# Moving the edge search for the last node tiles into the head of a graph layer, and starting its adding DMAs there

## The chip, the cores and the metric

The kernel runs on one core of one Trainium2 chip, as a single launch. The metric is the device time of one execution in microseconds (us); lower is better. Engines are named as the profile names them: PE (TensorE matmul), PEld (its weight loads), DVE (VectorE), ACT (ScalarE), POOL (GpSimd), and SP (SyncE), whose queue SPq issues most of the DMAs.

## The reference

One layer of a graph network on 3125 nodes with 256 channels and 103,125 directed edges (50,000 random pairs in both directions, and a loop on every node), sorted by destination. Cut to what matters:

```python
def _L0_gnn_ref(x, edge_index, ...):
    src, dst = (edge_index[0], edge_index[1])
    agg = jax.ops.segment_sum(x[src], dst, num_segments=N)     # N = 3125
    h = jax.nn.relu(agg @ W_rel + b_rel + x @ W_root)          # 256 -> 512
    gates = h @ W_ih.T + b_ih + b_hh
    i, f, g, o = jnp.split(gates, 4, axis=-1)
    c = jax.nn.sigmoid(i) * jnp.tanh(g)
    h_lstm = jax.nn.sigmoid(o) * jnp.tanh(c)
    return h_lstm @ W_fc + b_fc

xn = _layernorm(x, axis=-1)
x = x + gnn(xn, edges) + mix(xn)          # mix: k^T v per head over all nodes
x = x + ffn(_layernorm(x, axis=-1))       # top 2 of 8 experts, 256 -> 1024 -> 256, gelu
```

## The kernel before, in words

**Tiles.** The nodes lie in 25 tiles of 126 rows. The sum over edges is done in two ways. For the first 22 tiles (TA) it is a dense product: in the edge stage PE builds a 0/1 matrix `A` of source node by destination node, 252 destinations (a chunk) at a time, and multiplies the normalised nodes (as two parts, `hi` and `lo`) by it into `aggT`. A chunk has 14 builds: DVE writes two one-hot tiles `hr` and `hk` (line 477, two buffers each), PE multiplies them into a bank (483), ACT copies the bank into `A` (485). While the matmuls of one chunk run (796), the builds of the next are interleaved with them, bank by bank; there are 11 chunks, and `A0` for the first is built in the head.

For the last 3 tiles (TG) the sum is made by DMA: up to 60 times, for each tile, POOL issues an indirect DMA that gathers one source row for each of 126 nodes from `xn_dram` and adds it to an SBUF buffer (407, 180 such adds in all). Even ones add into `acc`, a view of `flat`, odd ones into `odds`.

**Head.** The nodes are loaded and normalised in five batches (`norm`), written to `xn_dram`, transposed (`turn`) and multiplied by W_root (`root`). Beside this, `find` looks up in the sorted edge list where the edges of each group of 6 nodes begin: DVE compares the first edges of all columns with the group's limit (282), POOL gathers the column found (290), DVE counts in it (296), POOL gathers 256 edges from there (305), and DVE turns them into keys (313 to 322) that are transposed for the builds. `find` is a generator that the code steps at chosen places.

**The last tiles' search.** `find_last` does the same for the 378 single nodes of the last three tiles: three compares over all columns (348), a gather (356), a check of the order of all edges (361, 362), three counts (366), a gather of 64 edges for each node (372), the hits (380), a PE matmul that adds up the counts of what went wrong (384), and the list `source` of rows to add (393 to 396). Before the change its first step stands at the end of the head, behind the last build of `A0` and the last `lo` split, and the other three in chunk 0 of the edge stage, beside banks 4, 8 and 10.

**Orders.** A scheduler places each engine's instructions; the code pins some of them. `then(ins, do, ...)` and `behind_(...)` run a step with its instructions queued behind given instructions on the same engine. In the edge stage a dictionary `queue` maps a chunk and a bank to the steps that stand beside it: the steps of the head mixer (`fetch`, which loads a batch `q` of `xn_dram` rows, `means`, `differences` and so on), `small_columns` and `router_rows`. In chunk 0 `fetch` stands at bank 7 and `means` (line 676, `hmean`) at bank 11, for the first batch. `next(adding)` issues an add beside some of the banks.

Of POOL's small work, `blank` (649, a row of zeros with an index in it) is stored by SP into `acc_dram` (652) and used for four fills of `xs_dram` (823); `heads` (640) masks the mixer's product; `tri`, `onesb`, `first`, `soon`, `token`, `valid`, `beyond` and `seen` serve the router.

**GNN chunks.** After the edge stage the nodes pass in seven chunks of up to four tiles (CUTS) through W_rel (1094), the gates (1104, four groups `m`), W_fc (1131) and the mixer's product (1134), then layer norms and the router, whose rows POOL scatters into `xs_dram` (1245). In each chunk the loop over `m` issues up to five adds per group, the first of which waits for the group's last matmul. The leftover adds are issued at the chunk that ends at tile 22 by `turned`: it adds `odds` to `acc` on DVE (1069), transposes the six blocks on PE (1073) and copies them on ACT into `accT`, which the last chunk reads in place of `aggT`. The experts' blocks (996, 1020) follow, and their rows are added into `out`.

Of the kernel before, what the change touches and what calls it, by code (L numbers as in the profile page):

```python
# [9 lines left out]
F32 = mybir.dt.float32  # L10
I32 = mybir.dt.int32
# [6 lines left out]
N = 3125  # L18
C = 256
# [20 lines left out]
TA = T - TG  # L40
GQ = 4
# [3 lines left out]
J = 60  # L45
SB = 256
# [24 lines left out]
def gps_layer(  # L71
# [21 lines left out]
    def ps_tr():  # L93
        return psum.tile([128, 512], F32, tag="tr", name="ps_tr", bufs=2)
# [42 lines left out]
    flat = main.tile([128, TG * C], F32, name="flat")  # L137
    acc = flat[:P].rearrange("p (m c) -> p m c", c=C)
    accT = flat[:, :KC * TG * P].rearrange("p (k n) -> p k n", k=KC)

    def agg_of(k, t0, t1):
        return aggT[:, k, t0 * P:t1 * P] if t0 < TA else accT[:, k, (t0 - TA) * P:(t1 - TA) * P]

# [99 lines left out]

    def find():
# [8 lines left out]
        for i in range(2):  # L253
            ends = sp.tile([128, NCP], F32, name="ends", tag="ends", bufs=3)
            nc.scalar.copy(ends, raw[:, i, :])
            for r in range(0, nr, 4):
                pt = ps_tr()
                m = min(4, nr - r)
                for j in range(m):
                    w = min(128, NCP - 128 * (r + j))  # L260
                    nc.tensor.transpose(pt[:w, 128 * j:128 * j + 128],
                                        ends[:, 128 * (r + j):128 * (r + j) + w], ident)
                whole_ = m if NCP >= 128 * (r + m) else m - 1
                if whole_:
                    nc.scalar.copy(rows[:, r:r + whole_, :, i],
                                   pt[:, :whole_ * 128].rearrange("p (r e) -> p r e", e=128))
                if whole_ < m:
                    nc.scalar.copy(rows[:left, r + whole_, :, i],
                                   pt[:left, whole_ * 128:m * 128])
# [10 lines left out]
        scr = sp.tile([128, NCP], F32, name="scr", tag="ends", bufs=3)  # L280
        for q in range(GQ):
            nc.vector.tensor_scalar(scr[:GP], firsts[:GP], limit[:, q:q + 1], None, op0=OP.is_lt, op1=OP.add,
                                    accum_out=below[:, q:q + 1])
# [11 lines left out]
        for q in range(GQ):  # L295
            nc.vector.tensor_scalar(scr[:GP, :128], near[:, q, :, 0], limit[:, q:q + 1], None,
                                    op0=OP.is_lt, op1=OP.add, accum_out=below[:, q:q + 1])
# [6 lines left out]
        for q in range(GQ):  # L304
            nc.gpsimd.indirect_dma_start(
                out=both[:, q].rearrange("p e o -> p (e o)"), out_offset=None,
                in_=ends_dram.rearrange("n e o -> (n e) o"),
                in_offset=bass.IndirectOffsetOnAxis(ap=begin_i[:, q:q + 1], axis=0))
        yield
# [30 lines left out]
    gathered = []  # L340

    def find_last():


        below = ep.tile([P, TG], F32, name="below2")
        for m in range(TG):
            scr = sp.tile([128, NCP], F32, name="scr2", tag="ends", bufs=3)
            nc.vector.tensor_scalar(scr[:P], firsts[:P], node[:, m:m + 1], None, op0=OP.is_lt,
                                    op1=OP.add, accum_out=below[:, m:m + 1])
        at = ep.tile([P, TG], F32, name="at2")  # L350
        nc.vector.tensor_scalar(at, below, -1.0, 0.0, op0=OP.add, op1=OP.max)
        at_i = ep.tile([P, TG], I32, name="at2_i")
        nc.vector.tensor_copy(at_i, at)
        near = ep.tile([P, TG, 128, 2], F32, name="near2")
# [5 lines left out]
        order = sp.tile([128, NCP], F32, name="order", tag="ends", bufs=3)  # L360
        nc.vector.tensor_tensor(order, raw[:, 0, :], behind, OP.is_gt)
        nc.vector.tensor_reduce(wrong[:, GQ:GQ + 1], order, AX.X, OP.add)
        yield
        hits = ep.tile([P, TG * JE], F32, name="hits2")
        for m in range(TG):
            nc.vector.tensor_scalar(hits[:, :128], near[:, m, :, 0], node[:, m:m + 1], None,
                                    op0=OP.is_lt, op1=OP.add, accum_out=below[:, m:m + 1])
        begin_i = ep.tile([P, TG], I32, name="begin2_i")
        nc.vector.scalar_tensor_tensor(begin_i, at, 128.0, below, op0=OP.mult, op1=OP.add)
        both = ep.tile([P, TG, JE, 2], F32, name="both2")  # L370
# [6 lines left out]
        yield  # L377
        mine = hits.rearrange("p (m e) -> p m e", e=JE)
        for m in range(TG):
            nc.vector.tensor_scalar(mine[:, m], both[:, m, :, 0], node[:, m:m + 1], None,  # L380
                                    op0=OP.is_equal)
        nc.vector.tensor_reduce(wrong[:P, GQ + 1:], mine[:, :, J], AX.X, OP.add)
        pw = ps_tr()
        nc.tensor.matmul(pw[:, :GQ + 2], ones, wrong, start=True, stop=True)
        total_f = const.tile([128, 1], F32, name="total_f")
        nc.vector.tensor_reduce(total_f, pw[:, :GQ + 2], AX.X, OP.add)
        off = const.tile([128, 1], F32, name="off")
        nc.vector.tensor_scalar(off, total_f, 1.0, float(FAR), op0=OP.min, op1=OP.mult)
        nc.vector.tensor_copy(total_i, total_f)
        yield  # L390


        nc.vector.scalar_tensor_tensor(mine, both[:, :, :, 1], -float(N), mine,
                                       op0=OP.add, op1=OP.mult)
        nc.vector.tensor_scalar(mine, mine, float(N), off[:P], op0=OP.add, op1=OP.add)
        nc.vector.tensor_scalar(source, mine, float(N), None, op0=OP.min)

    source = gw.tile([P, TG, JE], I32, name="source")

    def adds():  # L400

        for j in range(J):
            for m in range(TG):
                with ExitStack() as queued:
                    for one in added:
                        queued.enter_context(tc.issue_after(one.ins))
                    add = nc.gpsimd.indirect_dma_start(  # L407
                        out=(acc, odds)[j % 2][:, m, :], out_offset=None, in_=xn_dram[:, :],
                        in_offset=bass.IndirectOffsetOnAxis(ap=source[:, m, j:j + 1], axis=0),
                        compute_op=OP.add)  # L410
                added[:] = [add]
                yield add
# [84 lines left out]
    def then(ins, do, *of):  # L497

        with tc.issue_after(ins.ins):
            return do(*of)  # L500
# [20 lines left out]
    last = then(last, norm, 1)  # L521
    root(0)
    then(xts[-1][1], rounded, 0)
    then(last, next, steps)
    begun = pins.pop()
# [20 lines left out]
    keyed = pins.pop()  # L546
    listing = lambda: next(steps, None)
    root(3, *(GQ * [listing]))
    behind_((pins[0], evacs[-3]), norm, 4)
# [3 lines left out]
    one = lambda: next(parts)  # L553
    root(4, None, one, one)
    then(xts[-1][1], rounded, 4)
    next(parts)
    root(5, one, one, one)
    next(parts)
    stored = root(6, one, one, one)
    for part_ in parts:  # L560
        built = part_
    for b in range(2, T // TB):
        splits = then(built[1], split, b)
    last_steps = find_last()
    behind_((splits, built[1]), next, last_steps)
    found.close()
    nodes.close()
    adding = adds()

# [48 lines left out]
    odds = keep.tile([P, TG, C], F32, name="odds")  # L618
    for of in (acc, odds):
        nc.gpsimd.memset(of, 0.0)  # L620
# [18 lines left out]
    heads = keep.tile([128, 128], F32, name="heads")  # L639
    nc.gpsimd.memset(heads, 0.0)  # L640
    for i in range(128 // HC):
        nc.gpsimd.memset(heads[i * HC:(i + 1) * HC, i * HC:(i + 1) * HC], 1.0 / N)
# [3 lines left out]
    pkv = []  # L646

# [111 lines left out]
    queue = {(0, i): [(next, last_steps, None)] for i in (4, 8, 10)}  # L759
    queue[0, 9], queue[1, 3] = [(small_columns,)], [(router_rows,)]  # L760
    ADDS = 11
# [8 lines left out]
    with tc.tile_pool(name="odd", bufs=1) as op_:  # L770
        As = [A0, op_.tile([P, T, AC], F32R, name="A1")]
        for c, (d0, d1) in enumerate(chunks):
# [5 lines left out]
            def bank(i):  # L778
                built = next(parts, None)
                if built is None:  # L780
                    return
                with ExitStack() as queued:
                    for ins in built:
                        queued.enter_context(tc.issue_after(ins.ins))
                    for step, *of in queue.pop((c, i), ()):
                        step(*of)

                n = c * NB + i - ADDS
                if n >= 0 and n * 11 // 16 > (n - 1) * 11 // 16:
                    next(adding)  # L790
# [42 lines left out]
    with tc.If(total > 0):  # L833
        with tc.tile_pool(name="any", bufs=1) as ap_:
# [56 lines left out]
            nc.vector.tensor_tensor(acc, acc, ag, OP.add)  # L891
# [168 lines left out]
    with tc.tile_pool(name="gnn", bufs=1) as hp, tc.tile_pool(name="rt", bufs=2) as rp:  # L1060
# [4 lines left out]
        def turned():  # L1065

            for _ in adding:
                pass
            nc.vector.tensor_tensor(acc, acc, odds, OP.add)
            pts = [ps_tr() for _ in range(KC)]  # L1070
            for k in range(KC):
                for m in range(TG):
                    nc.tensor.transpose(pts[k][:, m * P:(m + 1) * P],
                                        acc[:, m, 128 * k:128 * k + 128], ident[:P, :P])
            for k in range(KC):
                nc.scalar.copy(accT[:, k, :], pts[k][:, :TG * P])

        def chunk(t0, t1, pending):
# [20 lines left out]
            for m in range(KH):  # L1099
# [10 lines left out]
                nc.scalar.activation(act[:, 1, :n], act[:, 0, :n], AF.Tanh)  # L1110
                nc.vector.tensor_tensor(hl[:, m, :n], act[:, 2, :n], act[:, 1, :n], OP.mult)
# [10 lines left out]
                if m == 2 and t1 == TA:  # L1122
                    with tc.issue_after(mm.ins):
                        turned()
# [357 lines left out]
```

## Time and profile before

| | us |
|---|---|
| median of 3 runs | 1094.63 |
| lowest and highest of them | 1090.86, 1095.67 |
| time of the profiled execution | 1092.31 |
| span in that execution's profile | 1090.5 |
| mean granted PE clock in it | 0.977 of full |

Stages in the profile: the head ends at 80.5 us, with the first matmul of the edge stage; the edge stage runs to about 320; the GNN chunks to about 710; the experts' blocks to the end.

The profile's lines give a start and a length in us, the engine, the source line, the operation and its tiles (output<-input), and in brackets the idle time of the engine just before, with what ended it. "SPq" and "POOLq" are the queues' own instructions. In tables by window the columns are the busy time of PE, PEld, DVE, ACT and POOL with counts, then the clock that PE was granted (PEclk, 1 is full), the share of the DMA engines and GB/s.

### The profile page before, as it was taken

Reading aid. Unit: us, or ns where it says so; the run is one execution under the profiler, and the core shown is the slowest. Engines: PE = TensorE matmul, PEld = TensorE weight load, DVE = VectorE, ACT = ScalarE, POOL = GpSimd, SP = SyncE. Lnnn points to the kernel's source line nnn. Section 1 sums busy time; section 2 is a strip of 40 time slices with the busy share of each in tenths; the row PEclk is TensorE's granted clock in tenths of the full one; section 3 lists DMA queues with packets and bytes.
Section 4 is the critical chain, followed back from the end, with each engine's and each line's share of the span. In section 5 each row is a group of like instructions: output and inputs, shape, how many; then the busy total and the mean of one; then the engine's idle time right before and its main releaser. Section 6 shows DMA issues by size and latency. Waiting matters only on the chain. (4 is left out here: it accounts for less than half of the span.)

```text
span 1090.5 us, 15243 instructions
## 1 busy us (share of the span) xinstructions
PE 1016.8 (93%) x5296; PEld 783.0 (72%) x5296; DVE 538.4 (49%) x1734; ACT 422.1 (39%) x918; POOL 563.8 (52%) x472
## 2 busy tenths in 40 slices
PE   6996999989999999999996899999999999999994
PEld 3466989889984545454553666788888888888883
DVE  5868778867831393929291734471112222222220
ACT  4462748467413242424351334542322222322221
POOL 2105888888706748787877030353443534344444
PEclk9998999999999999999998899999999999999997
DMA  8953999999624444966363210147767665766641
GB/s 269 312 182 85 246 288 295 283 216 277 99 115 106 78 108 82 270 118 128 78 128 79 70 60 15 54 158 254 241 223 253 215 223 203 264 217 210 205 149 41
DMA packets 142674, 188.03 MB, mean 172 GB/s; under 512 B 14371, under 2 KB 124978, under 8 KB 142462
## 3 DMA queue, kind: packets, MB, share of 16 engines
q1 hardware_dynamic: 103668, 140.56, 39.9%
q0 software_dynamic: 38080, 45.57, 21.0%
q8 instruction: 44, 0.72, 0.3%
q10 hardware_dynamic: 840, 0.83, 0.2%
q14 instruction: 42, 0.34, 0.1%
HBM read 128.72 MB, written 59.06 MB: 172 GB/s over the span
## 5 line engine op out<-in xcount | busy, mean ns | idle before, releaser
L1104 PE MATMUL ps_mm<-hT,wih 128*128 128x504 f32 (+1 forms) x672 | 258.8, 545 | 0.0
L1104 PEld LDWEIGHTS ps_mm<-hT,wih 128*128 128x128 f32 x672 | 127.5, 191 | 126.7 <-issue 90.2
L996 PE MATMUL ps_mm<-xe,w 128*128 128x256 f32 (+1 forms) x896 | 185.3, 364 | 0.0
L1020 PE MATMUL ps_o<-w,hf 128*128 128x256 f32 x832 | 184.9, 379 | 0.0
L407 POOL DMA_INDIRECT odds<-xn_dram,source x90 | 158.4, 1760 | 34.7 <-issue 25.2
L996 PEld LDWEIGHTS ps_mm<-xe,w 128*128 128x128 f32 x896 | 160.4, 190 | 20.3 <-issue 0.2
L407 POOL DMA_INDIRECT flat<-xn_dram,source x90 | 154.4, 1716 | 35.3 <-issue 24.9
L1020 PEld LDWEIGHTS ps_o<-w,hf 128*128 128x128 f32 x832 | 155.7, 190 | 19.9
L796 PE MATMUL ps_o<-A,hi 126*128 126x252 f32 x550 | 151.3, 308 | 0.6 <-ACT A L485 0.6
L998 ACT ACTIVATE hf<-ps_mm,sm 128x256 f32<-128x256 f32 (+1 forms) x160 | 72.3, 452 | 188.0 <-PE ps_mm L996 185.9
L796 PE MATMUL ps_o<-A,lo 126*128 126x252 f32 x550 | 137.6, 282 | 0.0
L485 ACT CAST A<-ps_mm 126x450 fp32r<-126x450 f32 x154 | 82.5, 536 | 96.2 <-PE ps_mm L483 94.5
L483 PE MATMUL ps_mm<-hk,hr 128*126 128x150 bf16 x924 | 93.0, 237 | 21.9 <-DVE hk L477 20.4
L974 POOL DMA_INDIRECT old<-out_dram,xs x52 | 53.7, 1032 | 112.3 <-issue 67.8
L796 PEld LDWEIGHTS ps_o<-A,hi 126*128 126x128 f32 x550 | 106.3, 193 | 2.6 <-ACT aggT L804 1.7
L796 PEld LDWEIGHTS ps_o<-A,lo 126*128 126x128 f32 x550 | 106.6, 194 | 0.0
L477 DVE TENSOR_TENSOR hr<-two,rowT 128x756 bf16<-128x756 bf16 x154 | 84.2, 547 | 42.4 <-PE ps_mm L483 41.7
L483 PEld LDWEIGHTS <-hr 128*126 128x126 bf16 x924 | 82.8, 141 | 30.1 <-DVE hk L477 26.4
L477 DVE TENSOR_TENSOR hk<-two,keyT 128x900 bf16<-128x900 bf16 x154 | 95.7, 621 | 0.0
L1106 ACT ACTIVATE act<-ps_mm,bg 128x504 f32<-128x504 f32 (+1 forms) x84 | 52.9, 634 | 104.7 <-PE ps_mm L1104 103.9
L1245 POOL DMA_INDIRECT xs_dram<-rows,at_i x50 | 50.7, 1013 | 65.3 <-DVE at_i L1243 50.0
L1023 DVE TENSOR_TENSOR y<-ps_o,b2s 128x256 f32<-128x256 f32 x52 | 22.0, 424 | 120.7 <-PE ps_o L1020 81.2
(290 smaller groups left out, 1149.9 us busy)
## 6 DMA issues: line engine op xcount, KB each, us to landing
w<-in_W_dram SPq DMA_DIRECT2D x56, 1024.0 KB
xs_dram<-blank SPq DMA_DIRECT2D x3, 7022.5 KB
xs_dram<-blank SPq DMA_DIRECT2D x1, 6757.5 KB
xs<-xs_dram SPq DMA_DIRECT2D x21, 265.0 KB
root_dram<-hr SPq DMA_DIRECT2D x8, 504.0 KB
root<-root_dram SPq DMA_DIRECT2D x4, 1008.0 KB
b2s<-in_b_dram SPq DMA_DIRECT2D x28, 128.0 KB
xn_dram<-xn SPq DMA_DIRECT2D x5, 630.0 KB
```

The lines of the kernel that those rows point to most:

```text
L407: add = nc.gpsimd.indirect_dma_start(out=(acc, odds)[j % 2][:, m, :], out_offset=None, in_=xn_dram[:, :], in_offset=bass.IndirectOffsetOnA ...
L477: row = nc.vector.tensor_tensor(to[:, :m], two[:, :, :w, :].to_broadcast([128, m, w, GH]), of[:, g:g + m, None, :].to_broadcast([128, m, w ...
L483: mm = nc.tensor.matmul(pa[:P, i * DT:(i + 1) * DT], hr[:, i, :, h], hk[:, i, :, h], start=(h == 0), stop=(h == GH - 1))
L485: copy = nc.scalar.copy(A[:, :, c0:c0 + m * D], pa[:P, :m * DT].rearrange("p (d t) -> p t d", t=T))
L796: last = nc.tensor.matmul(pg[k][:, :n], of[:, t, 128 * k:128 * k + 128], A[:, t, :n], start=(t == 0 and of is hi), stop=(t == T - 1 and of ...
L974: get = nc.gpsimd.indirect_dma_start(out=old[:, h, :], out_offset=None, in_=out[:most, :], in_offset=self.rows_(h), bounds_check=most - 1, ...
L996: mm = nc.tensor.matmul(pm, self.w1[:, k, 128 * m:128 * m + 128], self.xe[:, k, :], start=(k == 0), stop=(k == KC - 1))
L998: nc.scalar.activation(hf[:, m, :], pm, AF.Gelu, bias=b1s[:, m:m + 1])
L1020: mm = nc.tensor.matmul(po, hf[:, m, 128 * h:128 * h + 128], self.w2[:, m, :], start=(m == 0), stop=(m == KF - 1))
L1104: mm = nc.tensor.matmul(pm[:, :n], wih[:, k, i, 128 * m:128 * m + 128], hT[:, k, :n], start=(k == 0), stop=(k == KH - 1))
L1106: nc.scalar.activation(act[:, i, :n], pm[:, :n], AF.Tanh if gate == 2 else AF.Sigmoid, bias=bg[:, gate, m:m + 1])
L1245: put = nc.gpsimd.indirect_dma_start(out=xs_dram[:, :], out_offset=bass.IndirectOffsetOnAxis(ap=at_i[:, i:i + 1], axis=0), in_=rows[:, i, ...
```

## The change

- `find_last` is stepped from the head: its first step behind `norm(1)` and ahead of `find`'s second, its gather behind `find`'s gathers, its counts and second gather behind the keys and ahead of `norm(4)`, its last two steps beside builds 3 and 5 of `A0`; `split(2)` stands beside build 8, and splits 3 and 4 stay behind the last build. The scratch buffers of the searches are borrowed from `aggT`.
- `acc` holds both sums of each tile (six slots); it is cleared at the start of POOL's work. `odds`, `flat` and `accT` go.
- Six adds are issued before the edge stage, and then beside its banks from the first bank on, at 13 for 16 banks instead of 11 for 16 from bank 11 on.
- `turned` no longer adds on DVE. PE multiplies both sums of a tile with the identity into one accumulator, and ACT copies it into columns of `aggT` that were used up (WRAP). It stands behind the gates' last matmul, the last tanh and the last product of the chunk that ends at tile 22, instead of beside its third group.
- `heads` moves from the pool `keep` to the mixer's pool on the same side.

The diff, cut to its core:

```diff
+WRAP = max(t for t in CUTS if t <= TA)
+SUMS = 2
+NS = TG * SUMS
...
-    flat = main.tile([128, TG * C], F32, name="flat")
-    acc = flat[:P].rearrange("p (m c) -> p m c", c=C)
...
     def agg_of(k, t0, t1):
-        return aggT[:, k, t0 * P:t1 * P] if t0 < TA else accT[:, k, (t0 - TA) * P:(t1 - TA) * P]
+        w = WRAP if t0 >= WRAP else 0
+        return aggT[:, k, (t0 - w) * P:(t1 - w) * P]
+    acc = main.tile([P, NS, C], F32, name="acc")
+    nc.gpsimd.memset(acc, 0.0)
...
+    room = [NCP]
+    def borrowed(n):
+        room[0] += TG * n
+        return aggT.rearrange("p k n -> p (k n)")[:P, room[0] - TG * n:room[0]].rearrange(
+            "p (m n) -> p m n", m=TG)
+    def scratch(p, n=NCP):
+        return aggT.rearrange("p k n -> p (k n)")[:p, :n]
...
     def find_last():
...
-        nc.vector.tensor_copy(at_i, at)
-        near = ep.tile([P, TG, 128, 2], F32, name="near2")
+        yield nc.vector.tensor_copy(at_i, at)
+        near = borrowed(256).rearrange("p m (e o) -> p m e o", o=2)
         for m in range(TG):
             nc.gpsimd.indirect_dma_start(...)
+        yield
         order = ...
-        yield
...
-        yield
+        yield at_begin
...
         for j in range(J):
             for m in range(TG):
...
-                        out=(acc, odds)[j % 2][:, m, :], out_offset=None, in_=xn_dram[:, :],
+                        out=acc[:, m * SUMS + j % SUMS, :], out_offset=None, in_=xn_dram[:, :],
...
     last = then(last, norm, 1)
+    last_steps = find_last()
+    last = then(last, next, last_steps)
     root(0)
     then(xts[-1][1], rounded, 0)
     then(last, next, steps)
+    then(gathered[-1], next, last_steps)
...
-    keyed = pins.pop()
+    keyed = then(pins.pop(), next, last_steps)
...
-    behind_((pins[0], evacs[-3]), norm, 4)
+    behind_((keyed, pins[0], evacs[-3]), norm, 4)
...
+    beside = {3: [(next, last_steps)], 5: [(next, last_steps)], 8: [(split, 2)]}
+    def one():
+        built = next(parts, None)
+        if built is not None:
+            count[0] += 1
+            for do, *of in beside.get(count[0], ()):
+                behind_(built, do, *of)
+        return built
...
-    for b in range(2, T // TB):
-        splits = then(built[1], split, b)
-    last_steps = find_last()
-    behind_((splits, built[1]), next, last_steps)
+    for b in (3, 4):
+        then(built[1], split, b)
     found.close()
     nodes.close()
     adding = adds()
+    for _ in range(6):
+        next(adding)
...
-    odds = keep.tile([P, TG, C], F32, name="odds")
-    for of in (acc, odds):
-        nc.gpsimd.memset(of, 0.0)
...
-    heads = keep.tile([128, 128], F32, name="heads")
+    mix = ExitStack()
+    mp = mix.enter_context(tc.tile_pool(name="mix", bufs=2, side="right"))
+    heads = mp.tile([128, 128], F32, name="heads", bufs=1)
...
-    queue = {(0, i): [(next, last_steps, None)] for i in (4, 8, 10)}
-    queue[0, 9], queue[1, 3] = [(small_columns,)], [(router_rows,)]
-    ADDS = 11
+    queue = {(0, 9): [(small_columns,)], (1, 3): [(router_rows,)]}
...
-                n = c * NB + i - ADDS
-                if n >= 0 and n * 11 // 16 > (n - 1) * 11 // 16:
+                n = c * NB + i
+                if n * 13 // 16 > (n - 1) * 13 // 16:
                     next(adding)
...
-        def turned():
+        def turned(t0, ts):
             for _ in adding:
                 pass
-            nc.vector.tensor_tensor(acc, acc, odds, OP.add)
-            pts = [ps_tr() for _ in range(KC)]
             for k in range(KC):
-                for m in range(TG):
-                    nc.tensor.transpose(pts[k][:, m * P:(m + 1) * P],
-                                        acc[:, m, 128 * k:128 * k + 128], ident[:P, :P])
-            for k in range(KC):
-                nc.scalar.copy(accT[:, k, :], pts[k][:, :TG * P])
+                pt = ps_tr()
+                for i, t in enumerate(ts):
+                    m = t - TA
+                    of = [(m * SUMS + o, ident[:P, :P]) for o in range(SUMS)]
+                    for s, to in of:
+                        nc.tensor.matmul(pt[:, i * P:(i + 1) * P], acc[:, s, 128 * k:128 * k + 128],
+                                         to, start=(s == of[0][0]), stop=(s == of[-1][0]))
+                nc.scalar.copy(agg_of(k, ts[0], ts[-1] + 1), pt[:, :len(ts) * P])
+                if t0 < ts[0]:
+                    nc.vector.tensor_copy(agg_of(k, t0, ts[0]), aggT[:, k, t0 * P:ts[0] * P])
...
-                if m == 2 and t1 == TA:
-                    with tc.issue_after(mm.ins):
-                        turned()
+            ts_ = range(max(t1, TA), min(T, ([*CUTS, T])[CUTS.index(t1) + 1]))
+            if ts_:
+                behind_((mm, tanh, held), turned, t1, ts_)
```

## The prediction

> **What bounds the kernel now.** I read the page's share per engine first, then who makes TensorE (PE) wait, then the stretches in which it waits, then what the releasing engine was doing there.
>
> From the page, busy time per engine, and TensorE's waits (line that waits, releaser, us in total, times, longest):
>
> ```profile
> PE 1016.8 (93%) x5296; PEld 783.0 (72%) x5296; DVE 538.4 (49%) x1734; ACT 422.1 (39%) x918; POOL 563.8 (52%) x472
> ...
> PE ps_mm L483 <- DVE hk L477: 20.4, 17, 6.5
> PE ps_o L1131 <- DVE hl L1111: 13.8, 1, 13.8
> ```
>
> TensorE is the bound nearly everywhere. From 660 us on its tenths stand at 10 of 10 until the last scatter, so what is won or lost before 660 passes to the end one for one. Two waits stand out: 6.5 us behind the edge builds, and one of 13.8 us in the GNN chunks. The timeline of PE and DVE (start, length, what, idle before it) places both:
>
> ```profile
> 83.31 1.05 DVE L348 TENSOR_SCALAR_CACHE_REDUCE scr<-firsts,node 126x808 f32<-126x808 int32 x1
> 89.33 1.01 PE L483 MATMUL ps_mm<-hk,hr 128*126 128x150 bf16 x6 [6.45 <-DVE hk L477]
> ...
> 599.61 0.96 DVE L1069 TENSOR_TENSOR flat<-flat,odds 126x768 f32<-126x768 f32 x1 [18.39 <-DMA odds<-xn_dram,source]
> 602.69 1.22 PE L1131 MATMUL ps_o<-wfc,hl 128*126 128x256 f32 x2 [13.75 <-DVE hl L1111]
> ```
>
> The first is DVE working off three `lo` splits and `find_last` (79.1 to 88.7) before it builds again. The second is DVE standing 18.4 us at `acc + odds`, which waits for the last adding DMA; POOL issues that one at 594.6 only. After it the windows (PE, PEld, DVE, ACT, POOL busy, then PEclk) show half clock:
>
> ```profile
> 590.00:600.00 10.00, 0.00 (x0) 0.00 (x0) 0.39 (x1) 0.00 (x0) 5.06 (x5) 0.69 0.28 72
> 600.00:610.00 10.00, 7.31 (x27) 6.28 (x28) 4.18 (x11) 2.56 (x4) 0.00 (x0) 0.63 0.00 0
> ```
>
> The queues that matter for what follows, POOL, SP's queue and DVE:
>
> ```profile
> 83.50 0.32 POOL L649 MEMSET blank<- 128x265 f32 x1 [49.94 <-DMA bg<-in_b_ih_dram]
> 106.76 1.75 POOL L407 DMA_INDIRECT flat<-xn_dram,source  x1 [4.95 <-DVE source L396]
> 118.64 2.00 POOL L407 DMA_INDIRECT flat<-xn_dram,source  x1 [0.30 <-issue]
> ...
> 83.94 0.37 SPq L652 DMA_DIRECT2D acc_dram<-blank  x1
> 84.36 1.05 SPq L669 DMA_DIRECT2D q<-xn_dram  x2
> ...
> 106.91 1.48 DVE L676 TENSOR_REDUCE hmean<-q 126x40 f32<-126x1280 f32 x1
> 109.66 0.64 PE L483 MATMUL ps_mm<-hk,hr 128*126 128x150 bf16 x6 [1.00 <-DVE hk L477]
> ```
>
> Read them as a chain: POOL clears `blank`; 0.1 us later SP stores it into `acc_dram`; behind that in the same queue stand the two loads of `q`; DVE needs the first `q` for `hmean`, which it takes after the 12th build of chunk 0; TensorE's 13th bank needs the build after that. Today the chain has 20 us to spare.
>
> **The change, part by part.**
>
> *The search in the head.* Step 1 (three compares of 0.98, two small ones) is 3.2 us in DVE's gap of 4.89 us at 19.9 to 24.8: nothing. Its gathers go behind POOL's at 33.6, where POOL idles until 83.5, and nobody waits for them there. Step 3 (0.91 + 0.90 + 3 x 0.38 + 0.16 = 3.1) goes into the 2.83 us gap at 45.8; the 0.3 too many, and what it queues ahead of, the `keyT` copy and norm 4, are absorbed by the 1.4 us gap at 55.4. Steps 4 and 5 (0.9 and 1.1) and one split (1.43) go between builds; DVE idles 0.64 to 1.4 before each build and is two buffers ahead, so PE's root matmuls cover them; uncovered they would cost 3.4. On PE the sum of `wrong` costs 0.4 in a stretch that is 10 of 10 busy. Head: +0.4, bounds 0 and 3.8. SP reads `total_i` earlier, at about 67.4, with only the stores of a later chunk behind it: nothing.
>
> *After the head* DVE has two splits instead of three and no search: chunk 0's first build ends at about 83.4 instead of 89.2. PE waits some 0.9 us, not 6.45, and stays at full clock. Taken alone chunk 0 would end near 101.8 (80.9 + 0.9 + 20, the length of chunk 1, 112.5 to 133) instead of 112.5: -10.7.
>
> *The adding DMAs.* `source` comes after build 7. Its hr starts at 66.12 today; total_f, off, total_i and the last two operations bring `source` to 67.8, the first add to 68.1. Adds begin 39 us earlier, 119 stand before the GNN chunks (6 + 113) instead of 89, and the other 61 end at the start of chunk 3, near the place of today's 510 us. They leave the `acc + odds` wait for good.
>
> *What they stand in front of.* The changed program's instruction order shows this on POOL: 28 adds, then `heads`, `blank`, then the rest. `heads` and `blank` now share the right-hand pool and must wait for the head's buffers to come free; the adds don't, and so 28 were put ahead. SP still has `acc_dram<-blank` and then both `q`; DVE still has `hmean` after 12 builds. So I follow the chain: an add with its issue gap takes 1.90 (1.59 + 0.30, the quiet GNN chunks) to 1.98 (106.76 to 118.64 is six), 2.18 under the fills. Fills wait for chunk 0's end, so I take 1.92: 28 x 1.92 = 53.8, to 121.9; two memsets 0.45, to 122.4; store behind its semaphore 0.5, `q` issued at 122.9. Landing: a load of the same 630 KB in the head was issued at 27.94, and DVE got it at 32.90, 4.96; the `base` loads took 5.4 to 8.6. With 4.96, `hmean` starts at 127.9 instead of 106.91: +21.0 for bank 13 and all behind it (this contains the head's +0.4 and takes back the -10.7). By bounds: 1.88 per add and 3.9 (the three transfers of 1.4 MB at the highest rate, 364 GB/s, without latency) give +19; 2.18 and 7.8 give +31.
>
> The Trainium skill ("DMA: Bandwidth & Descriptors", Anatomy of one DMA) states about 2 us and bytes/436 GB/s for one transfer, 3.5 us here; by it the sum would be 1.5 us lower.
>
> PE then idles about 30 us (100 to 130) and comes back slow. Behind 13.75 us idle, PE's groups at 602.7 to 607.9 took 1.22, 1.06 and 3.33 where the next ones take 0.6, 0.6 and 1.89: 2.5 lost in 5 us. I take +2.6 here; below, 2.5; if the ramp grows with the idle, up to 5.
>
> The skill ("TensorE: Matmul & The Clock Gate", What's actually happening) says half clock follows one idle window of 3.4 us, and that one busy window lifts it. By that the loss would be 1.7 whatever the idle; the row shows more, and the row decides. It speaks against this change, which swaps two stalls for a longer one.
>
> *The joined sums.* DVE's 18.4 us wait goes. PE's 13.75 shrinks to what the next chunk shows there (2.12 for eight L1131 at 649.1 against 1.89): -13.5, and its slow clock -2.5. In place of six transposes (0.81 together at 640.8) PE does 12 f32 matmuls with 126 columns; nearest is L1134, two of 128 columns in 0.60, so 3.6: +2.8, bounds 0.8 and 3.6 more. They stand behind the last gate of chunk 5 now, ahead of its L1131, as do two ACT copies; 3.6 us of PE hides those. Together -13.2.
>
> Clearing the wider `acc` at POOL's start (1.46 instead of 0.73) delays `limit` to 3 us; DVE needs it at 5.5: nothing. From chunk 1 on, adds and fills end as far ahead of the stage's end as today (24 us), so DMA contention moves along.
>
> Sum: 21.0 + 2.6 - 13.2 = +10.4 on the profiled execution of 1092.31: 1102.7. The three other times have their median 2.3 above that execution; I lay half of this on it: 1104.
>
> **The rivals.**
>
> *The loads of q are there in time (faster).* Place: `hmean`, chunk 0. The balance is zero at hmean = 117.5 (106.9 + 13.2 - 2.6), that is at 1.55 us per add. Below that it is faster; with no wait at all -10.7 - 13.2 gives 1068 to 1070. Against it: no add in the page is below 1.58 + 0.30, and the chain reads the same in the order of both programs. For it: POOL's spans are rough, and adds in the quiet head have not been seen. Chance 0.12.
>
> *The stall is deeper.* Adds at 2.18 and a slow landing: +31 instead of 21, 1114. For: DVE's builds and the stores of the head run beside the first adds. Against: no fill is under way. Chance 0.12.
>
> *The wait at chunk 5 stays* in another form (the joined matmuls, or a POOL late through scatters): -13.2 becomes up to 0, 1117. Against: the last add moves by 85 us. Chance 0.04.
>
> *Other small waits end with the old ones* (PE lost about 5 us at 230 to 250 behind a `q` load, 2.6 at 572): 1098, no measurable change. Chance 0.10.
>
> **How the numbers follow.** Forecast 0.62, within 1099 to 1109 by the bounds of add, landing, clock and transposes. With the deeper stall below 1113 and the small waits down to 1095 the range 1095 to 1113 holds 8 in 10; left out are the faster case and the far ends. Half a per cent (5.5 us) is about what a measurement here can tell: slower by more 0.77 (forecast, deeper stall and 0.03 of the wait that stays), within it 0.11, faster 0.12.
>
> **What would show it.** In the changed profile: one PE wait near 100 to 130 us at the edge builds, released by DVE, with DVE waiting there for DMA `q`; POOL's `blank` at about 122; the first add near 68; PEclk below 1 after 130; no DVE wait for adds near 600, and `ps_o<-wfc,hl` with no wait over 1 us. Wrong is the forecast if `hmean` starts before 118, or if adds need under 1.6 us each.

## The result, and the profile after

The changed kernel takes 1109.49 us (median of 4 runs, 1105.92 to 1113.14), the kernel before 1094.14 beside it: a ratio of 1.0145, 95% interval 1.0101 to 1.0188. It is slower by 1.45%. Its profiled execution took 1107.72 us with a span of 1105.9, 15.4 longer than the span of before; TensorE worked as long as before (1016.3 us against 1016.8) and its mean clock fell from 0.977 to 0.967. Line numbers of the changed kernel are up to 35 higher.

The table of waits of the changed kernel (who waits, for whom, us in total, times, longest):

```profile
PE ps_mm L502 <- DVE hk L496: 52.5, 17, 35.2
...
DVE hmean L709 <- DMA q<-xn_dram: 42.1, 3, 34.5
```

Where before had two long waits of TensorE, 6.5 us at the builds and 13.8 in the GNN chunks, there is now one of 35.2 us, at the builds; the next longest is one of 7.4 in chunk 6 of the edge stage (5.0 before). The second line gives its cause: DVE, which makes the one-hot tiles, stood 34.5 us for a load of `q`. The timeline places it, in the order of the chain:

```profile
69.81 1.73 POOL L426 DMA_INDIRECT acc<-xn_dram,source  x1 [17.32 <-DVE source L413]
...
122.92 1.58 POOL L426 DMA_INDIRECT acc<-xn_dram,source  x1 [0.30 <-issue]
124.07 0.91 POOL L682 MEMSET blank<- 128x265 f32 x1
125.00 0.33 SPq L685 DMA_DIRECT2D acc_dram<-blank  x1
125.37 1.10 SPq L702 DMA_DIRECT2D q<-xn_dram  x2
131.68 1.49 DVE L709 TENSOR_REDUCE hmean<-q 126x40 f32<-126x1280 f32 x1 [34.47 <-DMA q<-xn_dram]
134.44 1.01 PE L502 MATMUL ps_mm<-hk,hr 128*126 128x150 bf16 x6 [35.18 <-DVE hk L496]
...
663.98 2.84 PE L1106 MATMUL ps_tr<-ident,acc 126*128 126x126 f32 x24
```

Read each start against the line above it: 28 adds from 69.81 to 124.5, `blank` behind the last of them (the two overlap a little, since POOL's spans are rough), the store 0.02 after `blank` ends, `q` right behind the store in SP's queue, `hmean` 6.31 after that, TensorE 2.76 later. Nothing in the chain has slack. The last line is the joined sums, with no wait ahead of it. Two windows (PE, PEld, DVE, ACT, POOL busy, PEclk, DMA share, GB/s):

```profile
110.00:120.00 10.00, 0.00 (x0) 0.00 (x0) 0.00 (x0) 0.00 (x0) 8.48 (x6) 0.50 0.51 68
130.00:140.00 10.00, 5.56 (x34) 5.51 (x35) 5.88 (x10) 1.82 (x4) 9.12 (x9) 0.57 0.76 135
```

In the first, PE, DVE and ACT have nothing at all; only POOL works, at its adds. In the second TensorE is back, at a granted clock of 0.57.

### The profile page after: what moved, and what is told of

Same layout as the page of the kernel before. It is cut to its first block, busy times and chain, and to the rows that moved or that the text cites. A ratio compares the mean times of both kernels' runs of the same rounds, so it can differ in the third digit from the quotient of the medians.

```text
span 1105.9 us, 15221 instructions
## 1 busy us (share of the span) xinstructions
PE 1016.3 (92%) x5314; PEld 784.5 (71%) x5314; DVE 536.9 (49%) x1733; ACT 423.3 (38%) x918; POOL 560.6 (51%) x471
## 5 line engine op out<-in xcount | busy, mean ns | idle before, releaser
L426 POOL DMA_INDIRECT acc<-xn_dram,source x180 | 310.5, 1725 | 82.3 <-issue 50.2
L504 ACT CAST A<-ps_mm 126x450 fp32r<-126x450 f32 x154 | 82.6, 537 | 124.5 <-PE ps_mm L502 122.8
L1062 POOL TENSOR_TENSOR old<-y,old 128x256 f32<-128x256 f32 x52 | 37.6, 723 | 86.8 <-DMA old<-out_dram,xs 57.5
```

The costliest lines, as they stand in the source:

```text
L426: add = nc.gpsimd.indirect_dma_start(out=acc[:, m * SUMS + j % SUMS, :], out_offset=None, in_=xn_dram[:, :], in_offset=bass.IndirectOffset ...
L504: copy = nc.scalar.copy(A[:, :, c0:c0 + m * D], pa[:P, :m * DT].rearrange("p (d t) -> p t d", t=T))
```

## The experiments

The theory to test is the prediction's: `q` stands behind the store of `blank`, that behind 28 adds, and the GNN wait went because the adds begin earlier and end earlier. "Old pace", "six ahead" and so on are short names of the kernels. Runs made together share the runs of the kernel before, whose median was 1098.84 beside the first four and 1100.26 beside the last four; so kernels are compared by their ratio to it.

### Six ahead: the chain cut on POOL

```diff
-    nc.gpsimd.iota(blank[:, C + NE:].bitcast(I32), pattern=[[0, 1]], base=N, channel_multiplier=1)
+    added.append(nc.gpsimd.iota(blank[:, C + NE:].bitcast(I32), pattern=[[0, 1]], base=N, channel_multiplier=1))
```

The next add, the seventh, is queued behind what stands in `added`, and so behind `heads` and `blank`.

> Only the place of 22 adds changes: POOL does 6 adds, then heads and blank, then the others. Queue theory (q stands behind the store of blank, and that behind 28 adds on POOL): blank is cleared near 84, q issued near 86, hmean does not wait, PE's wait of 35 us at the 13th bank goes, chunk 0 ends near 103.5 instead of 138.5, and with it the whole execution comes 35 us earlier: 1107.7 - 35 = 1072.7 (1067 if the 5 us that chunks 3 to 6 lost go too), 0.977 to 0.983 of before. Traffic theory (the early adds themselves slow the loads of q and the builds): the same adds run at the same times, so most of the wait stays, 1095 to 1108. Gain given back (a later wait takes the place of the one removed): 1085 to 1095.

Measured: 1081.0 us, ratio 0.986 (0.9808 to 0.9912). `blank` was cleared at 83.84, `q` issued at 87.11, `hmean` ran at 98.58 without a wait, and chunk 0 ended at 104.4 instead of 139.3. So the stall is the place of 22 adds on POOL: the same adds beside the same loads cost no such wait. But only 26 of the 35 us came through on the spans of the profiled executions (1105.9 and 1079.5; by the two ratios it is about 31). The timeline of six ahead, between the edge stage and the GNN chunks, shows where most of the rest stayed:

```profile
323.25 1.59 POOL L426 DMA_INDIRECT acc<-xn_dram,source  x1 [0.30 <-issue]
...
326.99 1.86 DVE L1130 TENSOR_TENSOR hT<-ps_mm,root 128x504 f32<-128x504 f32 x3 [10.91 <-SPq L864]
...
327.72 3.73 PE L1128 MATMUL ps_mm<-aggT,wrel 128*128 128x504 f32 x4 [4.81 <-DVE hT L1130]
```

The edge stage was over at 316.2, but POOL had 119 adds to work off ahead of the branch on `total` (line 864), until 324.84; SP and DVE go on 2 us after that, and TensorE waits for DVE. From the first W_rel matmul to the first gate it took 13.7 us instead of 6.9, which is 6.8 of the 9 us that are missing; from the first gate to the experts it took 3.2 more (354.6 for 351.4), which is not explained, while chunks 1 to 10 of the edge stage took 1.5 less. In the changed kernel the stall of 35 us had hidden this second limit: its adds ended at 319, the edge stage at 352.

### Seventeen ahead: the dose

`range(17)` early adds instead of `range(6)`, and the 18th queued behind `blank`.

> The dose: 17 adds ahead of heads and blank instead of 28. Queue theory: 11 adds of 1.9 us less, 20.9 earlier: hmean near 110.8 instead of 131.7, PE's wait at the 13th bank 35 - 21 = 14, time near 1087. Traffic theory: no change from 28 ahead, 1107. If the wait were set by something else that comes at 131 (a buffer, a semaphore of the head), hmean stays at 131.

The timeline of seventeen ahead, DVE and PE at the same place:

```profile
114.65 1.49 DVE L709 TENSOR_REDUCE hmean<-q 126x40 f32<-126x1280 f32 x1 [14.05 <-DMA q<-xn_dram]
...
117.41 1.01 PE L502 MATMUL ps_mm<-hk,hr 128*126 128x150 bf16 x6 [14.76 <-DVE hk L496]
```

TensorE waits 14.8 us (28 adds ahead: 35.2; 17: 14.8; 6: below 1); 11 adds fewer took 20.4 of it away, 1.86 each. The wait goes by the number of adds. The time (one run) missed: 1096.73 for 1087. The head of this run was 3.4 us longer (its edge stage begins at 85.53), and as the edit makes 17 + 113 = 130 adds stand before the branch, POOL ended them at 344 and the way from W_rel to the gates took 14.2.

### The store behind the fill: the chain cut on SP

```diff
-    with tc.issue_after(stored.ins):
-        nc.sync.dma_start(acc_dram[N:, :], blank[:, :C])
...
+                if c == 0:
+                    with tc.issue_after(fill.ins):
+                        nc.sync.dma_start(acc_dram[N:, :], blank[:, :C])
```

> POOL keeps its 28 adds ahead of blank; only SP's order changes: the store of blank into acc_dram goes behind the first fill of xs_dram, so that the two loads of q no longer stand behind it. Queue theory: blank still near 124, but q is issued near 83 and hmean does not wait; no PE wait of over 2 us in chunk 0, and the time is that of six ahead, 1067 to 1075, since the first fill comes at 125 instead of 105 and nobody waits for it. Traffic theory: q lands late beside the adds, and hmean waits for it still.

Half of it held. `hmean` ran at 99.42 without a wait while `blank` came at 128.40, so the store in SP's queue is the link. But the time (one run) was 1095.36: the wait came back one load later, as the timeline of this kernel shows:

```profile
130.53 24.41 SPq L858 DMA_DIRECT2D acc_dram<-blank  x1
...
167.89 4.82 SPq L700 DMA_DIRECT2D q<-xn_dram  x1
186.61 1.49 DVE L707 TENSOR_REDUCE hmean<-q 126x40 f32<-126x1280 f32 x1 [24.19 <-DMA q<-xn_dram]
189.37 1.01 PE L502 MATMUL ps_mm<-hk,hr 128*126 128x150 bf16 x6 [24.90 <-DVE hk L496]
```

The first fill of 7 MB waits for `blank` too and went out at 130 instead of 104. What stands behind it in SP's queue is held (the store itself took 24.41 us to issue), and so the third load of `q` went out at 167.89 instead of 143.09 in old pace. "Nobody waits for the fill" was wrong.

### Old pace: adds as before the change

```diff
-    for _ in range(6):
-        next(adding)
...
-                n = c * NB + i
-                if n * 13 // 16 > (n - 1) * 13 // 16:
+                n = c * NB + i - 11
+                if n >= 0 and n * 11 // 16 > (n - 1) * 11 // 16:
```

and `blank` queued ahead of the adds as in six ahead.

> heads and blank ahead of all adds, and the adds begun and spaced as before the change (from bank 11 on, 11 for 16 banks, none before the edge stage); the search stays in the head and TensorE still joins the sums. Theory of the second term: the last add comes 91 adds after the start of the GNN chunks again, PE waits for it at the joined sums of chunk 5, 10 to 11 us and 2.5 of slow clock, so the time is that of six ahead plus 13: near 1085. If the 5 us lost in chunks 3 to 6 come from the denser adds, they are back here and it is near 1080. Rival: the GNN gain comes from joining on TensorE, not from the earlier adds; then no wait appears and it equals six ahead, 1067 to 1074.

1073.2 us, ratio 0.9763 (0.9712 to 0.9815). It was to be 13 us slower than six ahead and is about 8 faster. The prediction's reason for the second term, the earlier adds, turns out not to be needed: with 91 adds left for the GNN chunks, as before the change, no wait appears. The timeline of old pace:

```profile
589.13 0.99 POOL L1278 DMA_INDIRECT xs_dram<-rows,at_i  x1 [0.30 <-issue]
590.42 1.63 POOL L426 DMA_INDIRECT acc<-xn_dram,source  x1 [0.30 <-issue]
...
629.86 2.84 PE L1104 MATMUL ps_tr<-ident,acc 126*128 126x126 f32 x24
```

The last add is issued behind eight scatters of rows on POOL, at 590.42, and is wanted at 629.86, 39 us later. So either TensorE's joining removed the wait, or the place of the joining.

### Before, with the addition later: place or engine

```diff
...
-                    with tc.issue_after(mm.ins):
-                        turned()
+                    behind_((mm, tanh, held), turned)     # still m == 2, t1 == TA
```

This is the kernel before. `tanh` and `held` are the group's last ACT and DVE instructions; before, only TensorE's matmul was named, which left DVE's `acc + odds` free to stand a chunk earlier in DVE's order.

> The kernel before with one edit: DVE's acc + odds is queued behind the third group's last product of the chunk that ends at tile 22, one chunk later in DVE's order than the profile of before has it (599.6 us). Adds begin and end as before, and DVE still does the addition. Place theory (the GNN wait came from where the addition stood in DVE's queue; the last add, behind eight scatters of rows on POOL, lands 35 us ahead of the first use of the sum): the 13.75 us wait and 2.5 us of slow clock go, 1092.3 - 16 = 1076, ratio 0.985. Theory of the prediction (the wait goes because adds begin earlier and end earlier): the wait stays or moves to the new place, 1088 to 1095, ratio 1. Theory that TensorE's joining is what removes it: the wait stays, ratio 1.

1082.65, ratio 0.9851 (0.981 to 0.9892): the expected ratio, from this one edit. The timeline of it (POOL, DVE):

```profile
597.98 1.79 POOL L407 DMA_INDIRECT odds<-xn_dram,source  x1 [0.30 <-issue]
...
632.01 0.95 DVE L1069 TENSOR_TENSOR flat<-flat,odds 126x768 f32<-126x768 f32 x1
```

The last add comes no earlier (597.98 against 594.62) and DVE still adds; the addition merely stands at 632 instead of 599.6, and waits for nothing. From the first gate to the first expert matmul it takes 352.4 us against 365.8 before and 351.4 in the changed kernel: this place gives 13.4 of the 14.4 us that the GNN stage gained, and the last 1.0 is less than the kernels with the later place differ by (351.4 to 355.4).

### Six ahead, fewer: the second cover

11 for 16 banks instead of 13 in six ahead; 102 adds stand before the branch.

> Six ahead with one number changed: 11 adds for 16 banks instead of 13, still from the first bank on, so about 101 adds stand before the GNN chunks instead of 119. Theory of the second cover (in six ahead POOL works its 119 adds off until 325 us, and all engines wait for it at the branch between the stages, 8 us): 101 adds end near 288, ahead of the edge stage's 316, the wait goes, and it equals old pace, 1070 to 1076. If early adds cost by their traffic, it stays near six ahead, 1079 to 1083.

1073.56, ratio 0.9754 (0.971 to 0.9799), equal to old pace. POOL's last add before the branch in this kernel:

```profile
288.22 1.60 POOL L426 DMA_INDIRECT acc<-xn_dram,source  x1 [0.30 <-issue]
```

It ends 28 us ahead of the edge stage (317.6), and from W_rel to the gates it takes 7.2. So 6.5 of the 7 us between the two were the wait for 119 adds, and the early start by itself shows neither a cost nor a gain.

### Fills later, and the sums by DVE again

```diff
-            i = FILL * c // 2
-            if c % 2 == 0 and i < nb:
+            i = FILL * (0, 2, 5, 6).index(c) if c in (0, 2, 5, 6) else nb
+            if i < nb:
```

on top of old pace.

> Old pace (heads and blank ahead of the adds, adds from bank 11 on at 11 for 16) with the third fill of xs_dram after chunk 5 instead of chunk 4, so that the last load of q goes out ahead of it. If the load of q behind a 7 MB fill is what PE waits for in chunk 6 (5.1 us of DVE, 5.7 of PE), the time falls by 4 to 5 us from old pace, to 1068 or 1069. If the load waits for its buffer or for the adds' traffic, nothing changes, 1073; if two fills in a row delay the first loads of the GNN chunks, slower, 1075 to 1085.

1069.32, ratio 0.9721 (0.9676 to 0.9766). The timeline of old pace first, then of fills later, for the last batch of `q`:

```profile
233.17 1.49 DVE L707 TENSOR_REDUCE hmean<-q 126x40 f32<-126x1280 f32 x1 [5.05 <-DMA q<-xn_dram]
...
235.92 1.01 PE L502 MATMUL ps_mm<-hk,hr 128*126 128x150 bf16 x6 [5.73 <-DVE hk L496]
```

```profile
184.61 22.38 SPq L700 DMA_DIRECT2D q<-xn_dram  x2
213.27 28.94 SPq L852 DMA_DIRECT2D xs_dram<-blank  x2
229.32 1.48 DVE L707 TENSOR_REDUCE hmean<-q 126x40 f32<-126x1280 f32 x1
```

(A row marked x2 joins two issues. The last load of `q` went out at 206.65, ahead of the third fill at 213.27.) The wait is gone, and chunk 6 takes 21.4 us instead of 28.4. Of these 7, about 4 reach the end: W_rel to the gates takes 8.6 instead of 6.9, for a reason that is open, and the head of this execution was 1.3 longer. The intervals of the two ratios overlap, so the 4 us rest on the traces.

The last kernel joins the sums by DVE, at the place of the experiment on before, and leaves TensorE one matmul for each block:

```diff
+        def summed():
+            for _ in adding:
+                pass
+            nc.vector.tensor_tensor(acc[:, ::SUMS, :], acc[:, ::SUMS, :], acc[:, 1::SUMS, :], OP.add)
...
-                    of = [(m * SUMS + o, ident[:P, :P]) for o in range(SUMS)]
+                    of = [(m * SUMS, ident[:P, :P])]
...
+                if m == 2 and t1 == TA:
+                    behind_((mm, tanh, held), summed)
```

> Fills later, and the two sums joined by DVE again (behind the third group's last product of the chunk that ends at tile 22), so that PE does 6 transposes instead of 12 matmuls. Prices: the 24 records of the joined sums took 2.84 us, six transposes 0.81, so 2.0 us less than fills later, near 1066. If the joined matmuls hid DVE's last product of the chunk, PE waits there instead and nothing is won. If TensorE's joining is what took the GNN wait away, a wait of over 10 us comes back, 1080.

1066.34, ratio 0.9695 (0.9654 to 0.9736), the lowest median, though its interval overlaps that of fills later. The timeline of it:

```profile
620.59 0.95 DVE L1097 TENSOR_TENSOR acc<-acc 126x768 f32<-126x768 f32 x1
...
626.93 1.50 PE L1107 MATMUL ps_tr<-ident,acc 126*128 126x126 f32 x12
```

The addition waits for nothing, and TensorE spends 1.50 us instead of 2.84 (not 0.81: these are f32 matmuls with the identity and take two records each, not the transposes of before). The 1.3 us are too small to be seen: the spans, 1067.9 and 1068.1, are equal. Which engine joins the sums makes no difference that these runs can tell.

## Why the prediction was right, point by point

The forecast was 1104 for 1109.49, inside the range of 1095 to 1113 and just above the 1099 to 1109 of the forecast itself. The direction and the chain behind the stall were right, and all that was to show it is in the trace; the reason given for the gain in the GNN chunks is not the one that the runs show (below). By its own steps, on the spans:

| step | predicted | measured |
|---|---|---|
| first matmul of the edge stage (head) | +0.4 | +1.6 |
| bank 13 of chunk 0, the head included | +21.0 | +24.8 |
| slow clock in chunk 0 | +2.6 | +1.8 |
| chunks 1 to 10 of the edge stage | 0 | +5.0 |
| GNN chunks | -13.2 | -14.4 |
| experts' blocks, to the end | 0 | -1.9 |
| sum, without the first row, which the second holds (0.2 lie between the stages; rounded) | +10.4 | +15.4 |

*The chain* was read rightly link by link; its sizes were low. The first add came at 69.81 for 68.1 and the adds at 1.97 apart for 1.92, so POOL was done at 124.5 for 121.9. The load of `q` took 6.31 from issue to DVE for 4.96. Two loads were issued together here, and adds ran beside them; which of the two made it longer is not shown. The estimate of 3.5 us by the Trainium skill ("DMA: Bandwidth & Descriptors", Anatomy of one DMA) is further off; that section fits its formula to DMAs issued by POOL, and these loads stand in SP's queue.

*The head.* +1.6 is not shown to be the change's: the kernel before with the later addition has the old head and began its edge stage at 82.04, against 80.51; kernels with the new head began between 82.1 and 85.5. What the search's move is worth is the chunk behind it. No run has it alone: old pace and before with the addition later differ in it, in the joining and in when the adds begin, and stand at 0.9763 and 0.9851, with intervals that just touch. From the start of the edge stage to the end of chunk 0 they took 20.8 and 31.8 us. The prediction's -10.7 for chunk 0 taken alone holds.

*The clock.* Chunk 0 ended 26.6 us later, 1.8 more than bank 13: after the idle, matmuls came 0.21 us apart instead of 0.115 until about 138.7, that is for 4.3 us, at a granted clock of 0.50. The prediction took 2.6 from the row at 602 us, against a rule of the Trainium skill ("TensorE: Matmul & The Clock Gate", What's actually happening: half clock until about 3.4 us of work) that gave 1.7 as an estimate. Here the estimate is nearer. The row was not misread: in before the granted clock is 0.50 from the restart at 602.69 to about 607.5, and 4.8 us at half clock are an estimated 2.4 lost, near the row's 2.5. Behind the 6.45 us wait at 89.33 it stays at 0.50 to about 95.5, for 6.2 us. So the slow stretch differs from stall to stall, and it was not longer behind the longest one (4.3 us behind 35.2 of idle, 4.8 behind 13.75, 6.2 behind 6.45): the fear that it grows with the idle did not come true.

*Chunks 1 to 10* were put at nothing. Chunk 6 took 2.8 us more and chunk 3 1.0, where TensorE's wait behind a load of `q` was 2.4 and 1.0 longer. Chunk 5 took 1.2 more with the same waits (the longest 1.75 us, 1.74 before); there the granted clock was 0.94 instead of 1.00. The load in chunk 6 waits behind a 7 MB fill, as fills later shows; that wait was in before too (4.4 us of DVE, now 6.7). The same ten chunks took 208.3 us in before, 210.6 in before with the addition later, 211.2 in old pace and 213.3 in the changed kernel. The first two have equal adds and fills, so about 2 of the 5 us lie within what such kernels vary by; why the others were lost stays open.

*The joined sums* had nearly the right size, but the reason given is not the one that the runs show. (Of the 1.2 us that the term was short, 0.8 is the price of the joined matmuls, 3.6 for a measured 2.84.) The text put the wait down to adds that begin late ("They leave the `acc + odds` wait for good", by the last add's moving 85 us). What the runs show is that DVE's addition stood a chunk too early in DVE's queue, ahead of a gate's product that TensorE's W_fc waited for; with the addition later, the last add, behind the scatters, could be as late as before. In the changed kernel the last add did come early, at 540.09, so by the times that alone should have ended the wait too; no run has earlier adds with the addition in its old place. The change did both, and the prediction did not credit the later place with anything: that its term held in spite of this is partly luck. Both times stand in the prediction: DVE adds at 599.6, and TensorE transposes the sum at 640.8. The timeline of before has the second:

```profile
640.84 0.81 PE L1073 MATMUL ps_tr<-ident,flat 126*128 126x126 f32 x6
```

The prediction did not ask why an addition may hold up DVE when nobody reads its result for 40 us.

*The rival with the loads in time* was priced at 1068 to 1070, and six ahead, which makes just that case, took 1081 (0.986). It lacked POOL's own account: 119 adds of some 2.1 us, begun at 70, end at 324, past the edge stage of 316. The text checked that adds end 24 us ahead of the stage's end, but in the forecast's case, where the stall makes the stage longer. Six ahead, fewer, in which POOL is done in time, took 1073.56.

So of the change's parts, the search in the head gains (11 us of chunk 0, by the traces), the later place of the joining gains (13.4 us), the denser and earlier adds gain nothing beside it, and they cost: 28 of them stand in front of a memset on which the loads of `q` depend through SP's queue. Without them, as in old pace, it is faster by 2.4%.

## What to carry to other kernels

Before work is added to a queue that looks idle, list what stands behind it there and follow each item to the queues of the other engines: here a 0.3 us memset on POOL held a store on SP, the loads behind that, DVE, and TensorE. When an engine waits at an instruction whose result is used much later, look at the place of that instruction before speeding up the producer. And when a stall is priced away, do the sum again for every engine that the stall had given time.

## What the runs showed of the hardware that was not expected

An instruction that only issues a DMA can itself take long: behind a 7 MB fill the next issue on SP's queue took 24.41 us (the store) or 20.39 (`wr_dram` in old pace). And the memset of `blank` took 0.32 us wherever it stood ahead of the adds or some us after one, and 0.91 in the three kernels in which it ran right behind a long row of them (the changed kernel, seventeen ahead, the store behind the fill).
